# Attention sums moved by DMA into a transposed tile and divided there; norms that add the negated mean

## The chip, the core and the metric

The kernel runs on one core of a Trainium2 chip. The metric is the device time of one execution in microseconds, as the median over runs. TensorE is called PE in the profile, VectorE DVE, ScalarE ACT, GpSimd POOL; SP is the queue of SyncE, which issues every DMA of this kernel.

## The reference

Eight batches of 512 tokens with 256 channels pass through two attention layers and, after each, a tree-shaped feed-forward layer, all in float32. Each of the four parts starts with a layer norm and is added to the stream. The second attention is causal and rotates its queries and keys.

```python
def _layernorm(x, axis=-1, eps=1e-05):
    m = jnp.mean(x, axis=axis, keepdims=True)
    v = jnp.var(x, axis=axis, keepdims=True)
    return (x - m) / jnp.sqrt(v + eps)

# attention a (b: no biases, rotated q and k, causal mask), 16 heads of 16 channels
qkv = (jnp.einsum('bne,fe->bnf', x, qkv_w) + qkv_b).reshape(b, n, 3, HEADS, HEAD_DIM)
q, k, v = (qkv[:, :, 0], qkv[:, :, 1], qkv[:, :, 2])
scores = jnp.einsum('bnhd,bmhd->bhnm', q, k) / jnp.sqrt(jnp.float32(HEAD_DIM))
attn = jax.nn.softmax(scores, axis=-1)
out = jnp.einsum('bhnm,bmhd->bnhd', attn, v).reshape(b, n, EMBED)
return jnp.einsum('bne,fe->bnf', out, out_w) + out_b

# feed-forward: 255 gates, 256 leaf probabilities as products along the paths of a tree
gate = jax.nn.sigmoid(q_flat @ routers.T)
leaf_prob = _leaf_probs(gate)
ret = (leaf_prob @ leaf_values).reshape(Bv, Tv, d)
return jnp.einsum('btd,ed->bte', ret, Wout_w) + Wout_b

x = x + attention_a(_layernorm(x))
x = x + ffn(_layernorm(x))
x = x + attention_b(_layernorm(x))
x = x + ffn(_layernorm(x))
```

## The kernel before

The whole stream lies in SBUF, one tile per batch. There are 16 sequences of work, numbered n: 0 to 7 are the first attention of batches 0 to 7, 8 to 15 the causal one. The 16 heads of a sequence are handled in four groups g of four heads j; a group's four heads use four strips of 32 rows of the array.

The main loop counts half-steps: 32 per sequence, for each group four key tiles kt (or query tiles) in two pairs of heads. In a half-step the program emits `scores` for two heads (st, line 371), the row `maxima` of a later group for two heads (mx, line 334, twelve half-steps ahead), the `exponentials` (pt, line 381, ACT), and in every other half-step `weigh` (av, line 390), which multiplies the weights by v, a key tile behind. In the causal half an `affine_select` on POOL (line 523) cuts the diagonal block of pt before `weigh` may read it. v carries ones in 16 of its 32 columns, so av holds, per head, 16 rows of sums and 16 rows of the softmax's denominator.

`maxima` reduces each mx on DVE into a tile called less. When a group's less is complete, `put` transposes it (lessT, line 355), negates it on ACT (rows) and sends it by four small DMAs (q<-rows, line 360) into row 16 of each strip of q; the scores of that group then subtract the maximum by themselves, and must wait for these DMAs.

At a group's last key tile `weigh` copies av to SBUF (o, line 396), and a unit `divide` follows: four transposes on TensorE bring it to tokens by channels (oT, line 407), DVE takes the reciprocal of the denominators (inv, line 411) and multiplies (out, line 413). After the fourth group `post` transposes the whole of out back (outTp, line 245, 2 x 4 transposes with a copy on ACT to outT), multiplies it by the output weights (y, line 254) and adds it to x on DVE (line 423). Then `tree` runs the feed-forward layer: a norm, transposes (txt), gates (z), the products lp on DVE, transposes (lt), the leaves (ty), and an add to x.

`layer_norm` takes statistics on DVE (lines 224 and 225) and finishes on POOL: eps is added (line 229), the power taken (line 230), and four instructions form xn (line 233) as (x - mean) * rstd. `pre` is the front of the next sequence: norm, transposes (xt), q and k (line 282), rotation on POOL in the causal half (lines 302 to 306), DMAs that spread q and k over the strips (lines 294 and 310), and v.

Units are generators: each yields the kind of slot that it wants next ("pe" or "v") and a delay in half-steps. One unit of each kind is pulled per half-step, urgent ones first. On top of that a scheduler fixes each engine's final order when the program is built, so that an engine's order can differ from the program's. Each engine, SP's queue among them, takes its instructions in this order, and one that waits holds all behind it. SP's DMAs use eight semaphores in turn, and each waits for the eighth before it. PSUM has seven banks in rotation and one for av.

Of the kernel before, what the change touches and what calls it, by code (L numbers as in the profile page):

```python
# [31 lines left out]
F32 = mybir.dt.float32  # L35
AF = mybir.ActivationFunctionType
ALU = mybir.AluOpType
# [3 lines left out]
P = 128  # L41
B, S, D = 8, 512, 256
H, HD = 16, 16
NG, NJ = 4, 4
NT = S // P
NC = D // P
# [55 lines left out]
def hybrid_kernel(ctx, tc, x, a_qk, a_v, a_o, a_qk_b, a_v_b, a_o_b, b_q, b_k, b_v, b_o,  # L102
                  f_q, f_routers, f_values, f_out, f_out_b, cos, sin, leaf_scale, out):
    nc = tc.nc
# [27 lines left out]
    ident = const.tile([P, P], F32, tag="ident", name="ident")  # L132
# [19 lines left out]
    pool1 = ctx.enter_context(tc.tile_pool(name="w1", bufs=1))  # L152
    pool2 = ctx.enter_context(tc.tile_pool(name="w2", bufs=2))
# [5 lines left out]
                          (f_values, "f_values", "lp"), (f_out, "f_out", "lpT"))  # L159
    ]  # L160
    banks = ctx.enter_context(tc.tile_pool(name="banks", bufs=7, space=PSUM))
    ps_av = ctx.enter_context(tc.tile_pool(name="ps_av", bufs=1, space=PSUM))

    def bank(shape, name):
        return banks.tile(shape, F32, tag="ps", name=name)
# [11 lines left out]
    ks, vs, qs, outs, avs, lesses = [], [], {}, {}, {}, {}  # L177
    for i in range(2):
        k = pool1.tile([P, NG, S], F32, tag=f"k{i}", name=f"k{i}")
        v = pool1.tile([P, NT, H, 2 * HD], F32, tag=f"v{i}", name=f"v{i}")  # L180
# [5 lines left out]
    units = Units()  # L186
# [31 lines left out]
    def layer_norm(b, name, got):  # L218

        x = xs[b]  # L220
        stats = pool2.tile([P, NT, 6], F32, tag="ln_stats", name=f"ln_stats{name}")
        mv = pool2.tile([P, NT, 2], F32, tag="ln_mv", name=f"ln_mv{name}")
        for t in range(NT):
            nc.vector.bn_stats(stats[:, t, :], x[:, t, :])
            nc.vector.bn_aggr(mv[:, t, :], stats[:, t, :])  # L225
            if t % 2:
                yield "v", 0
        rstd = pool2.tile([P, NT], F32, tag="ln_rstd", name=f"ln_rstd{name}")
        nc.gpsimd.tensor_scalar(rstd, mv[:, :, 1], EPS, None, ALU.add)  # L229
        nc.gpsimd.tensor_tensor(rstd, rstd, neg_half, ALU.pow)  # L230
        xn = pool2.tile([P, NT, D], F32, tag="xn", name=f"xn{name}")
        for t in range(NT):
            nc.gpsimd.tensor_scalar(  # L233
                xn[:, t, :], x[:, t, :], mv[:, t, 0:1], rstd[:, t : t + 1], ALU.subtract, ALU.mult
            )
        got.append(xn)

# [3 lines left out]
    def transposed(dst, src, c, name):  # L241

        ps = bank([P, NT, P], name)
        for t in range(NT):
            nc.tensor.transpose(ps[:, t, :], src[:, t, c * P : (c + 1) * P], ident)  # L245
        nc.scalar.copy(dst[:, c, :], ps.rearrange("p t q -> p (t q)"))  # L246

    def by_tokens(srcT, w, n, tt, name):

        ps = bank([P, 2, D], name)  # L250
        for i in range(2):
            t = 2 * tt + i
            for c in range(NC):
                nc.tensor.matmul(  # L254
                    ps[:, i, :n], lhsT=srcT[:, c, t * P : (t + 1) * P], rhs=w[:, c, :],
                    start=c == 0, stop=c == NC - 1,
                )
        return ps

    def pre(n):  # L260

        causal, b = divmod(n, B)
        w = wb if causal else wa
        got = []
        yield from layer_norm(b, f"n{n}", got)
        xn = got[0]
        xnT = pool2.tile([P, NC, S], F32, tag="xnT", name=f"xnT{n}")
# [115 lines left out]
    def weigh(n, g, kt, pt):  # L383

        if kt == 0:
            avs[n, g] = ps_av.tile([P, S], F32, tag="av", name=f"av{n}_{g}")
        av = avs[n, g]
        first = kt * P if n >= B else 0
        for j in range(NJ):
            nc.tensor.matmul(  # L390
                av[32 * j : 32 * j + 32, first:], lhsT=vs[n % 2][:, kt, g * NJ + j, :],
                rhs=pt[:, j, : S - first], start=kt == 0, stop=kt == NT - 1,
            )
        if kt == NT - 1:
            o4 = pool2.tile([P, S], F32, tag="o4", name=f"o4{n}_{g}")
            nc.scalar.copy(o4, avs.pop((n, g)))
            units.add(divide(n, g, o4), "pe", 1, urgent=True)

    trees = {}

    def divide(n, g, o4):

        if g == 0:
            outs[n] = pool1.tile([P, NT, D], F32, tag="out", name=f"out{n}")
        ps = bank([P, NT, NJ, 2 * HD], f"oT{n}_{g}")
        for t in range(NT):
            nc.tensor.transpose(  # L407
                ps[:, t, :, :].rearrange("p j d -> p (j d)"), o4[:, t * P : (t + 1) * P], ident
            )
        inv = pool2.tile([P, NT, NJ, 1], F32, tag="inv", name=f"inv{n}_{g}")  # L410
        nc.vector.reciprocal(inv, ps[:, :, :, HD : HD + 1])
        to = outs[n].rearrange("p t (g j d) -> p t g j d", g=NG, j=NJ)
        nc.vector.tensor_tensor(
            to[:, :, g, :, :], ps[:, :, :, 0:HD], inv.to_broadcast([P, NT, NJ, HD]), ALU.mult
        )
        if g == NG - 1:
            trees[n] = units.add(post(n), "pe", 1)
        return
        yield

    def add_to_x(b, ps, tt):
        part = xs[b][:, 2 * tt : 2 * tt + 2, :]
        nc.vector.tensor_tensor(part, ps, part, ALU.add)  # L423

    def post(n):

        causal, b = divmod(n, B)
        outT = pool1.tile([P, NC, S], F32, tag="outT", name=f"outT{n}")
        out = outs.pop(n)
        for c in range(NC):  # L430
            transposed(outT, out, c, f"outTp{n}_{c}")
            yield "pe", 0
        for tt in range(NT // 2):
            add_to_x(b, by_tokens(outT, (wb if causal else wa).o, D, tt, f"y{n}_{tt}"), tt)
            yield ("v", 1) if tt else ("pe", 0)
        yield from tree(n, b)

    def tree(n, b):

        got = []
        yield from layer_norm(b, f"t{n}", got)
        xn = got[0]
        xnT = pool2.tile([P, NC, S], F32, tag="xnT", name=f"txnT{n}")
# [40 lines left out]
    def place(i, swapped):  # L486
        n, i = divmod(i, STEPS)
        g, i = divmod(i, 2 * NT)
        u, pair = divmod(i, 2)
        return n, g, u, pair ^ swapped  # L490
# [8 lines left out]
    for i in range(-LEAD, total + 2):  # L499
        ahead = i + LEAD  # L500
        if ahead < total:
            n, g, u, pair = place(ahead, 1)
# [15 lines left out]
        if got is not None:  # L518
            exponentials(sn, kt, got, pt)
            if sp == 1:  # L520
                if sn >= B:

                    nc.gpsimd.affine_select(  # L523
                        out=pt[:, :, :P], in_=pt[:, :, :P], pattern=[[0, NJ], [1, P]],
# [3 lines left out]
        if i % 2 and (len(waiting) > 1 or (i >= total and waiting)):  # L528
            weigh(*waiting.popleft())
# [64 lines left out]
```

## Time and profile before

| | |
|---|---|
| time, median of 3 runs | 1599.61 us (1596.56 to 1602.42) |
| the profiled execution | 1595.46 us |
| its span, first to last instruction | 1593.7 us |
| mean granted clock of TensorE | 0.862 of full speed |
| PE busy | 1481.2 us (93%) |
| DVE, ACT, POOL busy | 757.5, 665.9, 453.8 us |
| DMA traffic of the queue q1 | 24736 packets, 29.64 MB |

The page gives for each engine the time in which it had an instruction at work, and a picture of the span in 40 slices, each digit a share in tenths. PEclk is the clock that TensorE was granted. A row of a group of instructions ends with the mean ns of one, the idle time just before them and what ended it. A row of waits reads: who waited, at which line, for whom; total us, times, longest. A row of the timeline reads: start, length, engine, line, operation, output and inputs, how many in a row, and in brackets the idle time before it with its releaser. A window row gives its length, the busy us and count of PE, PEld, DVE, ACT and POOL, then the granted clock, the DMA share and GB/s.

### The profile page before, as it was taken

To read this page: it belongs to the slowest core of one execution; us is meant where nothing else is said; L and a number is where in the kernel's file an instruction comes from. 1 tells how busy PE (TensorE), PEld (TensorE's weight loads), DVE (VectorE), ACT (ScalarE), POOL (GpSimd) and SP (SyncE) were. 2 spreads that over 40 slices of the span, in tenths; PEclk is the share of its full clock that TensorE was granted. 3 is DMA by queue.
4 is the path that set the end of the run, shared out by engine and by line. 5 is a ranking of instruction groups with operands and counts; after the bars stand their busy time and mean duration, and the time that the engine had idled before them with its cause. 6 is when DMAs were issued, how large, how long until landed. Compare 5 with 4: busy or idle time off the path is not lost.

```text
span 1593.7 us, 22833 instructions
## 1 busy us (share of the span) xinstructions
PE 1481.2 (93%) x8276; PEld 668.1 (42%) x8276; DVE 757.5 (48%) x2247; ACT 665.9 (42%) x1443; POOL 453.8 (28%) x452
## 2 busy tenths in 40 slices
PE   4999999999999999999998898989889798989895
PEld 2333444334344434433444444445445343445444
DVE  2355655546546555455544343544444344544422
ACT  1155545445445444545454342534334343433331
POOL 7000300402104040032416245451624445251312
PEclk9599999889799988979999596977979787986767
DMA  7001001000010100100101000000101001010000
GB/s 230 17 11 18 11 1 27 2 17 12 2 27 1 28 1 1 28 1 8 22 1 28 1 14 15 23 19 14 28 1 32 10 23 19 15 28 2 14 14 13
DMA packets 24847, 31.09 MB, mean 20 GB/s; under 512 B 4000, under 2 KB 16032, under 8 KB 24736
## 3 DMA queue, kind: packets, MB, share of 16 engines
q1 hardware_dynamic: 24736, 29.64, 7.9%
q8 instruction: 66, 1.08, 0.3%
q14 instruction: 45, 0.37, 0.1%
HBM read 8.13 MB, written 4.19 MB: 8 GB/s over the span
## 4 chain that ended last, share of the span: by engine, by line
PE 84%; POOL 7%; DVE 6%; issue 1%; ACT 1%; DMA 1%; SPq 0%; POOLq 0%; DVEq 0%; ACTq 0%
PE st L371 26%; PE av L390 15%; PE mx L334 10%; PE qk L282 8%; PE z L254 5%; PE ty L254 4%; PE v L254 4%; PE y L254 4%; DVE lp L471 3%; POOL xnt L233 2%; POOL xnn L233 2%; PE oT L407 2%; PE txt L245 2%; PE lt L245 2%; PE outTp L245 1%
## 5 line engine op out<-in xcount | busy, mean ns | idle before, releaser
L381 ACT ACTIVATE pt<-st 128x512 f32<-128x512 f32 (+3 forms) x1024 | 473.7, 517 | 488.1 <-PE mx L334 413.8
L334 PE MATMUL mx<-k,q 16*128 16x512 f32 (+3 forms) x2048 | 623.5, 631 | 6.1 <-issue 6.1
L371 PE MATMUL st<-q,k 17*128 17x512 f32 (+3 forms) x2048 | 565.2, 619 | 33.4 <-DMA q<-rows 29.6
L348 DVE TENSOR_REDUCE less<-mx 128x1 f32<-128x512 f32 x512 | 328.5, 684 | 301.0 <-PE mx L334 300.3
L343 DVE CUSTOM_DVE_ANT_0 seen<-mx,mask 128x512 f32<-128x512 f32 (+3 forms) x512 | 230.7, 487 | 340.5 <-PE mx L334 331.2
L390 PE MATMUL av<-pt,v 128*32 128x512 f32 (+3 forms) x2048 | 272.3, 608 | 27.9 <-POOL pt L523 27.8
L371 PEld LDWEIGHTS st<-q,k 17*128 17x128 f32 x2048 | 183.6, 208 | 232.9 <-issue 152.2
L334 PEld LDWEIGHTS mx<-k,q 16*128 16x128 f32 x2048 | 219.5, 209 | 58.5 <-ACT pt L381 28.5
L523 POOL TENSOR_SCALAR_AFFINE_SELECT pt<-pt 128x512 f32<-128x512 f32 x128 | 81.6, 640 | 431.8 <-ACT pt L381 431.1
L229 POOL TENSOR_SCALAR ln_rstdt<-ln_mvt 128x4 f32<-128x4 f32 x16 | 3.7, 232 | 592.9 <-DVE ln_mvt L225 592.9
L390 PEld LDWEIGHTS av<-pt,v 128*32 128x32 f32 x2048 | 43.0, 115 | 199.8 <-issue 139.5
L254 PE MATMUL z<-wg,txnT 128*128 128x255 f32 x256 | 79.7, 466 | 0.5 <-ACT txnT L246 0.5
L233 POOL TENSOR_SCALAR xnt<-x,ln_mvt,ln_rstdt 128x256 f32<-128x256 f32 x64 | 77.4, 1221 | 0.3
L233 POOL TENSOR_SCALAR xnn<-x,ln_mvn,ln_rstdn 128x256 f32<-128x256 f32 x64 | 77.4, 1220 | 0.1
L254 PE MATMUL ty<-wl,lpT 128*128 128x256 f32 x256 | 73.1, 436 | 0.0
L254 PEld LDWEIGHTS z<-wg,txnT 128*128 128x128 f32 x256 | 57.2, 235 | 35.6 <-issue 10.9
L282 PE MATMUL qk<-xnT,a_qk 128*128 128x512 f32 x128 | 68.0, 661 | 0.0
L254 PEld LDWEIGHTS ty<-wl,lpT 128*128 128x128 f32 x256 | 52.5, 216 | 32.0 <-DVE x L423 8.3
L471 DVE SCALAR_TENSOR_TENSOR lp<-th,lp 128x8 f32<-128x8 f32 (+6 forms) x224 | 64.0, 322 | 3.3
L302 POOL TENSOR_TENSOR by_cos<-eo,cos 128x512 f32<-128x512 f32 x32 | 40.7, 1270 | 80.4 <-ACT eo L287 80.4
L407 PE MATMUL oT<-ident,o 128*128 128x128 f32 x256 | 47.2, 313 | 10.6 <-DVE less L343 7.8
L407 PEld LDWEIGHTS oT<-ident,o 128*128 128x128 f32 x256 | 30.4, 155 | 58.6 <-ACT pt L381 20.9
(74 smaller groups left out, 1143.8 us busy)
## 6 DMA issues: line engine op xcount, KB each, us to landing
x<-x SPq DMA_DIRECT2D x8, 512.0 KB
q<-r SPq DMA_DIRECT2D x32, 128.0 KB
k<-r SPq DMA_DIRECT2D x32, 128.0 KB
q<-rows SPq DMA_DIRECT2D x256, 2.0 KB
q<-rot SPq DMA_DIRECT2D x64, 64.0 KB
k<-rot SPq DMA_DIRECT2D x64, 64.0 KB
out<-x SPq DMA_DIRECT2D x8, 512.0 KB
a_qk<-a_qk SPq DMA_DIRECT2D x1, 512.0 KB
```

What stands on the lines that cost most here:

```text
L233: nc.gpsimd.tensor_scalar(xn[:, t, :], x[:, t, :], mv[:, t, 0:1], rstd[:, t : t + 1], ALU.subtract, ALU.mult)
L254: nc.tensor.matmul(ps[:, i, :n], lhsT=srcT[:, c, t * P : (t + 1) * P], rhs=w[:, c, :], start=c == 0, stop=c == NC - 1,)
L282: nc.tensor.matmul(ps, lhsT=wt[:, k, c * P : (c + 1) * P], rhs=xnT[:, k, :], start=k == 0, stop=k == NC - 1,)
L334: nc.tensor.matmul(ps[:, :width], lhsT=qs[n][rows, g, qt * P : (qt + 1) * P], rhs=ks[n % 2][rows, g, :width], start=True, stop=True,)
L343: nc.vector.tensor_tensor_reduce(out=seen[:, :width], in0=ps[:, :width], in1=mask[:, S - width :], scale=1.0, scalar=LOWEST, op0=ALU.add, ...
L348: nc.vector.tensor_reduce(at, ps, AX.X, ALU.max)
L371: nc.tensor.matmul(ps[:, : S - first], lhsT=ks[n % 2][rows, g, kt * P : (kt + 1) * P], rhs=qs[n][rows, g, first:], start=True, stop=True,)
L381: nc.scalar.activation(pt[:, j, :width], ps[:, :width], AF.Exp, scale=SCALE)
L390: nc.tensor.matmul(av[32 * j : 32 * j + 32, first:], lhsT=vs[n % 2][:, kt, g * NJ + j, :], rhs=pt[:, j, : S - first], start=kt == 0, stop= ...
L407: nc.tensor.transpose(ps[:, t, :, :].rearrange("p j d -> p (j d)"), o4[:, t * P : (t + 1) * P], ident)
L471: nc.vector.scalar_tensor_tensor(pairs[:, :, :, side], of_level, one, lp, ALU.add, ALU.mult)
L523: nc.gpsimd.affine_select(out=pt[:, :, :P], in_=pt[:, :, :P], pattern=[[0, NJ], [1, P]], compare_op=ALU.is_ge, fill=0.0, base=0, channel_m ...
```

## The change

`weigh` no longer hands o to a unit on TensorE. It allocates three tiles per sequence, outT (channels by tokens, two halves c), den of the same shape, and few, and issues eight DMAs per group: for each head, one that folds the 512 denominators of one row into 16 partitions of 32 (few), and one that copies the 16 rows of sums to their place in outT. After the second and the fourth group a unit `divide` takes the reciprocal of few on DVE, writes it to a DRAM tile by one DMA (apart), and reads it back by eight DMAs, each of which spreads one head's 512 reciprocals over 16 partitions (den). One slot later POOL multiplies outT by den in place. `post` then starts with the output product. The transposes oT and outTp, the copies to outT and the products on DVE are gone.

In `layer_norm` a new POOL instruction forms the negated mean, and xn is computed as (x + negated mean) * rstd.

The lines of the file after move down by two to six.

```diff
+    dram = ctx.enter_context(tc.tile_pool(name="apart", bufs=2, space=bass.MemoryType.DRAM))
...
+        less_mean = pool2.tile([P, NT], F32, tag="ln_less", name=f"ln_less{name}")
+        nc.gpsimd.tensor_scalar(less_mean, mv[:, :, 0], -1.0, None, ALU.mult)
         rstd = pool2.tile([P, NT], F32, tag="ln_rstd", name=f"ln_rstd{name}")
...
             nc.gpsimd.tensor_scalar(
-                xn[:, t, :], x[:, t, :], mv[:, t, 0:1], rstd[:, t : t + 1], ALU.subtract, ALU.mult
+                xn[:, t, :], x[:, t, :], less_mean[:, t : t + 1], rstd[:, t : t + 1], ALU.add, ALU.mult
             )
...
             nc.scalar.copy(o4, avs.pop((n, g)))
-            units.add(divide(n, g, o4), "pe", 1, urgent=True)
+            if g == 0:
+                outs[n] = [pool1.tile([P, NC, S], F32, tag=t, name=f"{t}{n}") for t in ("outT", "den")]
+                outs[n].append(pool2.tile([P, NC, S // HD], F32, tag="few", name=f"few{n}"))
+            outT, den, few = outs[n]
+            c = g // 2
+            for j in range(NJ):
+                to = slice((g % 2) * 64 + HD * j, (g % 2) * 64 + HD * (j + 1))
+                nc.sync.dma_start(few[to, c, :], o4[32 * j + HD : 32 * j + HD + 1, :])
+                nc.sync.dma_start(outT[to, c, :], o4[32 * j : 32 * j + HD, :])
+            if g % 2:
+                units.add(divide(n, c), "v", 2, urgent=True)
...
-    def divide(n, g, o4):
-
-        if g == 0:
-            outs[n] = pool1.tile([P, NT, D], F32, tag="out", name=f"out{n}")
-        ps = bank([P, NT, NJ, 2 * HD], f"oT{n}_{g}")
-        for t in range(NT):
-            nc.tensor.transpose(
-                ps[:, t, :, :].rearrange("p j d -> p (j d)"), o4[:, t * P : (t + 1) * P], ident
-            )
-        inv = pool2.tile([P, NT, NJ, 1], F32, tag="inv", name=f"inv{n}_{g}")
-        nc.vector.reciprocal(inv, ps[:, :, :, HD : HD + 1])
-        to = outs[n].rearrange("p t (g j d) -> p t g j d", g=NG, j=NJ)
-        nc.vector.tensor_tensor(
-            to[:, :, g, :, :], ps[:, :, :, 0:HD], inv.to_broadcast([P, NT, NJ, HD]), ALU.mult
-        )
-        if g == NG - 1:
+    def divide(n, c):
+        outT, den, few = outs[n]
+        inv = pool2.tile([P, S // HD], F32, tag="inv", name=f"inv{n}_{c}")
+        nc.vector.reciprocal(inv, few[:, c, :])
+        apart = dram.tile([H // NC, S], F32, tag="apart", name=f"apart{n}_{c}")
+        nc.sync.dma_start(apart.rearrange("h (a r) -> (h a) r", a=HD), inv)
+        for h in range(H // NC):
+            nc.sync.dma_start(den[HD * h : HD * (h + 1), c, :], apart[h : h + 1, :].to_broadcast([HD, S]))
+        yield "v", 2
+        nc.gpsimd.tensor_tensor(outT[:, c, :], outT[:, c, :], den[:, c, :], ALU.mult)
+        if c == NC - 1:
             trees[n] = units.add(post(n), "pe", 1)
...
-        outT = pool1.tile([P, NC, S], F32, tag="outT", name=f"outT{n}")
-        out = outs.pop(n)
-        for c in range(NC):
-            transposed(outT, out, c, f"outTp{n}_{c}")
-            yield "pe", 0
+        outT = outs.pop(n)[0]
```

More of the change, by code (lines that the diff above doesn't have):

```diff
@@ L396, in weigh @@
             nc.scalar.copy(o4, avs.pop((n, g)))
-            units.add(divide(n, g, o4), "pe", 1, urgent=True)
-    trees = {}
-    def divide(n, g, o4):
-        if g == 0:
-            outs[n] = pool1.tile([P, NT, D], F32, tag="out", name=f"out{n}")
-        ps = bank([P, NT, NJ, 2 * HD], f"oT{n}_{g}")
-        for t in range(NT):
-            nc.tensor.transpose(
-                ps[:, t, :, :].rearrange("p j d -> p (j d)"), o4[:, t * P : (t + 1) * P], ident
-            )
-        inv = pool2.tile([P, NT, NJ, 1], F32, tag="inv", name=f"inv{n}_{g}")
-        nc.vector.reciprocal(inv, ps[:, :, :, HD : HD + 1])
-        to = outs[n].rearrange("p t (g j d) -> p t g j d", g=NG, j=NJ)
-        nc.vector.tensor_tensor(
-            to[:, :, g, :, :], ps[:, :, :, 0:HD], inv.to_broadcast([P, NT, NJ, HD]), ALU.mult
-        )
-        if g == NG - 1:
+            if g == 0:
[9 more added lines that the diff above has]
+                units.add(divide(n, c), "v", 2, urgent=True)
+    trees = {}
+    def divide(n, c):
[9 more added lines that the diff above has]
+        if c == NC - 1:
             trees[n] = units.add(post(n), "pe", 1)
-        return
-        yield
     def add_to_x(b, ps, tt):
```

## The prediction

> **What bounds the kernel now.** I read the page's busy rows first, then TensorE's own waits, then the stretches where it waits. PE is TensorE, PEld its weight loads, DVE VectorE, ACT ScalarE, POOL GpSimd, SP the queue that issues every DMA.
>
> ```profile
> PE 1481.2 (93%) x8276; PEld 668.1 (42%) x8276; DVE 757.5 (48%) x2247; ACT 665.9 (42%) x1443; POOL 453.8 (28%) x452
> PE   4999999999999999999998898989889798989895
> PEclk9599999889799988979999596977979787986767
> ...
> PE st L371 <- DMA q<-rows: 29.6, 7, 4.4
> PE av L390 <- POOL pt L523: 27.8, 8, 5.2
> ```
>
> TensorE is the bound: full through the first, non-causal half, full but for some 10% in the causal half. What it waits for there is named in the two rows (total us, times, longest): a row of negated maxima that comes by DMA, and pt behind POOL. The window table gives 702.66 us busy of 770 from 750 to 1520. One causal sequence shows both waits:
>
> ```profile
> 861.15 6.10 SPq L310 DMA_DIRECT2D k<-rot  x8
> 867.29 20.45 SPq L360 DMA_DIRECT2D q<-rows  x5
> 868.70 4.84 POOL L233 TENSOR_SCALAR xnt<-x,ln_mvt,ln_rstdt 128x256 f32<-128x256 f32 x4
> 871.64 1.19 PE L371 MATMUL st<-q,k 17*128 17x512 f32 x1 [4.21 <-DMA q<-rows]
> 881.31 1.93 PE L390 MATMUL av<-pt,v 128*32 128x512 f32 x8 [3.65 <-POOL pt L523]
> ```
>
> The fourth q<-rows DMA stood in SP's queue behind eight k<-rot DMAs, and TensorE stood 4.21 us. Then pt's affine_select stood on POOL behind 15 us of norms, and TensorE stood 3.65 us. So two in-order queues, SP and POOL, set the stalls, and the change puts work into both.
>
> A gap costs more than its length:
>
> ```profile
> 410.00:415.00 5.00, 5.00 (x32) 2.40 (x30) 2.60 (x15) 2.66 (x5) 0.00 (x0) 1.00 0.00 2
> 415.00:420.00 5.00, 4.24 (x32) 1.75 (x24) 5.00 (x10) 2.23 (x4) 0.00 (x0) 0.93 0.00 0
> 420.00:425.00 5.00, 5.00 (x24) 1.43 (x20) 1.79 (x4) 1.67 (x3) 0.00 (x0) 0.50 0.00 0
> 435.00:440.00 5.00, 5.00 (x20) 1.63 (x18) 1.36 (x3) 1.44 (x3) 0.00 (x0) 0.52 0.01 3
> 440.00:445.00 5.00, 5.00 (x30) 2.78 (x28) 2.67 (x4) 1.08 (x2) 0.00 (x0) 1.00 0.00 0
> ```
>
> The column after POOL's is the granted clock. After 0.76 us of idle it is 0.50 for some 20 us. In windows of 2 us nearly every stretch with 1.2 us or more of idle in the causal half is followed by 14 to 30 us at 0.5; some such stretches also begin with no gap.
>
> **The change, part by part.** The sum is made against the profiled execution, 1595.46 us (span 1593.7, 1.8 around it); the median of the runs is 4.1 us above it.
>
> *Removed.* 256 oT and 128 outTp transposes:
>
> ```profile
> L407 PE MATMUL oT<-ident,o 128*128 128x128 f32 x256 | 47.2, 313 | 10.6 <-DVE less L343 7.8 <-DVE less L348 1.4 <-ACT o L396 1.2
> L245 PE MATMUL outTp<-ident,out 128*128 128x128 f32 x128 | 21.8, 296 | 0.0
> L360 SPq DMA_DIRECT2D q<-rows x256: 572/573/968, 68.2 to 1530.4; - x128
> ```
>
> 47.2 + 21.8 = 69.0 us of TensorE, 4.3 us per sequence (16 of them), all on the path in the first half. The ACT copies to outT (18.8 us) and the DVE products (27.2 us) go too, but those engines are half idle, so they count nothing. In the last sequence the cover of TensorE is gone, and there the old route was short: o copied at 1554.5, y begun at 1557.4.
>
> *Added on SP.* Eight DMAs per (n, g), nine per (n, c): 512 + 288 = 800, beside 448 of its kind now (256 rows, 64 r, 128 rot). At the row's 573 ns (600 on average in a run of four) that is 460 us of issuing, in bursts of 4.8 us and 5 us, each ahead of some q<-rows. From issue to landing no row gives a plain number. Bounds: four rows issued from 402.01 move their bytes from 403 to 406, so about 2 us; the one behind k<-rot took 4.3; the final 512 KB store issued at 1589.96 was awaited 2.3 us. I take 2.
>
> *c = 0, first half.* In DVE's order the reciprocal stands before the last reduction of less_3, so lessT_3 on TensorE waits for it, and it for the four few DMAs. Let o be copied at T. SP issues few and outT in turn; the last few starts at T+3.7 and lands at T+5.7; reciprocal 0.25, reduction 0.68: lessT_3 at T+6.8. TensorE, with the transposes gone and xt moved elsewhere, has two half-steps of st and mx (1.0 each), one av (1.06) and half of another, and DVE its lp work: about T+4.4. Stall 2.4. Behind it SP: apart T+6 to 6.6, landed at 8.6; eight dens to 13.4; four rows, the first landed at T+15.5. st_3_0 is reached near T+14: 1.5 more.
>
> *c = 1, first half.* k<-r and three of four rows go before the dens; the last den lands near T+17, POOL's product (1.27, by the row by_cos, 128x512) ends at T+18.5, and y is reached between T+16 and T+18. I take 1 us, bounds 0 and 2.7. The norm after it starts later: 0.5.
>
> *Causal.* c = 0: the reciprocal holds the same reductions, and POOL's product stands before the affine_select of pt_2_2, waiting for the dens: 3.5 us. c = 1: SP's order is one q<-rot (waits for POOL's rot, T+3), eight few and outT (to T+8), seven q<-rot (to T+13), apart, three rows, eight dens (T+16 to T+20.6), the fourth row. The product ends at T+23; TensorE is at y near T+14: 9 us, where now there are 4.2. Then POOL has y's norm, the bias and the next norm ahead of pt_1_1: 2.2 + 15.7 us (0.5 of it the two new less_mean instructions at 0.23) against 10.5 us of TensorE work at about 0.9 clock: 6.4, where now there are 3.6. So +5 and +2.8.
>
> *The negated mean.* xn takes 1221 ns for 256 columns. The nearest rows say that the kind of operation does not matter: rot by subtract 1266, by add 1267. I take no change. [...] If add leaves the slow route, an estimate at the affine_select's 640 ns is 0.58 x 4 = 2.3 us per norm, two norms per causal sequence: up to -35.
>
> *Clock.* [...] The trace decides: gaps from 1 us on, 20 us at half, so 10 us of full-speed work where TensorE is the bound. In the first half the c = 0 stall is such a gap in each sequence and the c = 1 stall in about half; the present slow stretches (106 us from 150 to 750, 8 us lost per sequence) are partly replaced: +6. In the causal half already 39 of 93 us are slow: +3.
>
> Sum: first half 8 x (-4.3 + 3.9 + 1.5 + 6) = +57. Causal 7.5 x (-4.3 + 3.5 + 5 + 2.8 + 3) = +75. End: o to y by the new route is 4.8 + 2 + 0.3 + 2.6 + 4.8 + 2 + 1.3 - overlaps of 1.7 = 16 us against 3, the clock aside: +12 net of the transposes. +144: 1739; with the 4.1 us to the median 1743, said as 1740.
>
> **The rivals.** *Faster: the chains hide.* The c = 0 wait decides from the point where TensorE takes longer than 6.8 us from o to lessT_3. At half clock it takes 8.8, st_3_0 moves back too, and the removed transposes count. If slow stretches or later DVE work cover these places, what is left is -69 + 12: 1543. For it: DVE had been busy without a break around such a place (513.6 to 523.1). Against: the granted clock is 0.92 from 150 to 750, and the causal waits are there already. Chance 0.09.
>
> *No clock price.* The stalls come, but the stretches at half clock only move: 8 x 1.1 + 7.5 x 7 + 12 = +73: 1673. For it: slow stretches begin at 234 and 310 without a gap. Chance 0.22.
>
> *The negated mean pays.* All as forecast and -35: about 1705; with no clock price 1638. [...] against it rot. Chance 0.2.
>
> *About the same.* Hidden chains in the first half and longer stalls in the causal half cancel: 0.03. The forecast itself: 0.46.
>
> **How the numbers follow.** 1740 is the likeliest case. The low end takes in no clock price with the negated mean; the high end has two slow stretches per first-half sequence (+8 each) and 5 more in the causal ones: 1840. Range 1625 to 1840; the faster case lies outside. What a measurement of this kernel can tell from no change is about 0.3%, 5 us. Slower 0.88, same 0.03, faster 0.09.
>
> **What would show it.** In the profile after: oT and outTp gone; 800 more SP issues; TensorE waiting for lessT_3 behind DVE's inv, for st_3_0 behind rows, for y behind POOL's product; a lower PEclk in the first half; xn still at 1.22 us. Wrong would be: few landing within 3 us of o's copy, den within 12, no y waits over 2 us in causal sequences, or a clock of 0.92 or more in the first half.

## The result, and the profile after

The changed kernel takes 1755.82 us (median of 4 runs, 1738.66 to 1766.08), beside 1601.01 us (1596.56 to 1624.03) for the kernel before on the same chip. The ratio is 1.094, 95% interval 1.084 to 1.105. The profiled execution is the longest of the four, 1766.08 us (span 1764.4); its granted clock is 0.765, where the others have 0.77 to 0.78. Some executions of a kernel run over 1.5% longer at a lower granted clock (of 15 of the kernel before, the longest 1624.44 us at 0.841, the shortest 1580.69 at 0.872); medians here are over all executions and ratios over the others alone, so that a ratio is not the quotient of two medians.

From the page, TensorE's busy row and two rows of the 40 slices:

```profile
PE 1606.3 (91%) x7892; PEld 679.2 (38%) x7892; DVE 736.6 (42%) x2151; ACT 650.4 (37%) x1411; POOL 419.4 (24%) x516
...
PE   5999999999999999999998888989888897989984
...
PEclk8555969769797886888968686676878777787576
```

TensorE has 384 instructions fewer and is busy 125 us longer. In the first half it is as full as it was, in digits all 9, but PEclk now falls in the middle of the nines. That is the reading to learn: a busy row says that there was an instruction, not how fast it ran.

TensorE's waits (total us, times, longest), and those of the reciprocal:

```profile
PE av L395 <- POOL pt L529: 49.0, 22, 4.0
PE y L259 <- POOL outT L427: 41.7, 9, 14.0
...
PE lessT L360 <- DVE less L348: 16.5, 7, 3.1
...
PE lessT L360 <- DVE less L353: 7.1, 5, 2.9
...
PE st L376 <- DMA q<-rows: 0.5, 2, 0.4
```

```profile
DVE inv L421 <- DMA few<-o: 92.7, 24, 11.9
```

The waits that the prediction named are there, lessT behind DVE and y behind POOL's product; the one for q<-rows has gone (29.6 us before). But windows of 2 us show that between 150 and 750 us TensorE is idle for 6.1 us only (2.8 before), while the clock there is 0.803 (0.920 before): 118 us of full-speed work are lost to it, where 48 were.

Where that happens is seen by listing TensorE's instructions other than st, mx and av. First the kernel before, a timeline and windows of 5 us (the columns as above, the clock third from the end):

```profile
485.75 2.00 PE L254 MATMUL y<-a_o,outT 128*128 128x256 f32 x8
...
495.11 0.66 PE L407 MATMUL oT<-ident,o 128*128 128x128 f32 x4
...
502.78 0.66 PE L245 MATMUL txt<-ident,xnt 128*128 128x128 f32 x4
```

```profile
490.00:495.00 5.00, 5.00 (x32) 1.53 (x28) 4.41 (x10) 2.76 (x5) 4.16 (x6) 1.00 0.00 0
495.00:500.00 5.00, 5.00 (x35) 2.01 (x33) 3.46 (x7) 2.58 (x5) 5.00 (x5) 1.00 0.00 0
500.00:505.00 5.00, 5.00 (x32) 1.90 (x28) 2.59 (x5) 2.96 (x7) 5.00 (x4) 1.00 0.02 5
```

Then the kernel after, the same place of a sequence:

```profile
532.19 2.86 PE L259 MATMUL y<-a_o,outT 128*128 128x256 f32 x12
...
540.30 1.12 PE L376 MATMUL st<-q,k 17*128 17x512 f32 x2 [0.41 <-DVE less L353]
...
550.14 1.12 PE L250 MATMUL txt<-ident,xnt 128*128 128x128 f32 x4
...
558.30 2.92 PE L259 MATMUL z<-wg,txnT 128*128 128x255 f32 x8
```

```profile
534.00:539.00 5.00, 5.00 (x34) 2.07 (x33) 4.84 (x16) 1.62 (x3) 0.28 (x2) 1.00 0.00 0
539.00:544.00 5.00, 4.59 (x24) 1.30 (x23) 4.46 (x11) 2.17 (x4) 4.72 (x7) 0.92 0.10 21
544.00:549.00 5.00, 5.00 (x21) 1.68 (x17) 2.39 (x4) 2.31 (x5) 4.65 (x8) 0.50 0.05 11
549.00:554.00 5.00, 5.00 (x24) 1.95 (x16) 0.80 (x3) 1.29 (x3) 2.40 (x2) 0.50 0.00 1
554.00:559.00 5.00, 5.00 (x20) 1.49 (x19) 1.96 (x4) 2.03 (x4) 0.00 (x0) 0.50 0.00 0
559.00:564.00 5.00, 5.00 (x24) 3.25 (x22) 1.29 (x2) 1.68 (x3) 0.00 (x0) 0.88 0.00 0
```

From the end of y (535) to the first txt (550) TensorE executes st, mx and av alone (and one lessT, a narrow one): products that the trace shows as `17*128` (st), `16*128` (mx) and `128*32` (av), where y and txt are `128*128`. Eight microseconds into this stretch the clock halves, 3 us after one idle of 0.41 us, and it is full again only in z, 17 us later, though TensorE is busy for 5.00 of 5 us. In the kernel before, oT stands in the middle of the same stretch. Call the instructions of `128*128` (y, z, ty, qk, v and the 128 x 128 transposes) whole-array work. From 170 to 760 us of the changed kernel's trace eleven stretches between whole-array work are 13 us or longer, and the clock falls in all eleven.

The other unexpected line is in the norms (the kernel before had 77.4 us and 1221 ns in each such row):

```profile
L238 POOL TENSOR_SCALAR xnt<-x,ln_lesst,ln_rstdt 128x256 f32<-128x256 f32 x64 | 34.9, 558 | 1.8
```

### The profile page after: what moved, and what is told of

The parts are those of the page before. It is cut to its first block, busy times and chain, and to the rows that moved or that the text cites. A ratio compares the mean times of both kernels' runs of the same rounds, so it can differ in the third digit from the quotient of the medians.

```text
span 1764.4 us, 23322 instructions
## 1 busy us (share of the span) xinstructions
PE 1606.3 (91%) x7892; PEld 679.2 (38%) x7892; DVE 736.6 (42%) x2151; ACT 650.4 (37%) x1411; POOL 419.4 (24%) x516
## 4 chain that ended last, share of the span: by engine, by line
PE 74%; SPq 8%; DMA 5%; DVE 5%; POOL 5%; issue 2%; ACT 1%; ACTq 0%; DVEq 0%; POOLq 0%
PE st L376 24%; PE av L395 13%; PE mx L339 9%; PE qk L287 5%; PE ty L259 5%; PE y L259 4%; PE z L259 4%; PE v L259 3%; SPq L315 2%; DVE lp L477 2%; SPq L410 2%; PE lt L250 2%; DMA apart<-inv 2%; SPq L425 2%; PE txt L250 2%
## 5 line engine op out<-in xcount | busy, mean ns | idle before, releaser
L339 PE MATMUL mx<-k,q 16*128 16x512 f32 (+3 forms) x2048 | 683.9, 700 | 8.9 <-DMA k<-r 8.4
L376 PE MATMUL st<-q,k 17*128 17x512 f32 (+3 forms) x2048 | 637.0, 689 | 6.9 <-DVE less L348 3.8
L395 PE MATMUL av<-pt,v 128*32 128x512 f32 (+3 forms) x2048 | 311.6, 686 | 49.1 <-POOL pt L529 49.0
L376 PEld LDWEIGHTS st<-q,k 17*128 17x128 f32 x2048 | 202.6, 226 | 280.0 <-issue 158.7
L339 PEld LDWEIGHTS mx<-k,q 16*128 16x128 f32 x2048 | 234.9, 227 | 73.9 <-issue 31.6
L427 POOL TENSOR_TENSOR outT<-outT,den 128x512 f32<-128x512 f32 x32 | 41.0, 1282 | 696.6 <-DMA q<-rows 315.3
L259 PE MATMUL y<-b_o,outT 128*128 128x256 f32 x128 | 53.1, 575 | 37.8 <-POOL outT L427 37.8
L259 PEld LDWEIGHTS ty<-wl,lpT 128*128 128x128 f32 x256 | 60.6, 249 | 44.0 <-issue 11.3
L433 DVE TENSOR_TENSOR x<-y,x 128x512 f32<-128x512 f32 x32 | 22.0, 688 | 89.9 <-PE y L259 89.8
L433 DVE TENSOR_TENSOR x<-ty,x 128x512 f32<-128x512 f32 x32 | 22.1, 692 | 88.3 <-PE ty L259 88.3
L259 PEld LDWEIGHTS y<-b_o,outT 128*128 128x128 f32 x128 | 34.8, 290 | 57.2 <-POOL outT L427 45.3
```

Of the source, the lines that this page charges most:

```text
L259: nc.tensor.matmul(ps[:, i, :n], lhsT=srcT[:, c, t * P : (t + 1) * P], rhs=w[:, c, :], start=c == 0, stop=c == NC - 1,)
L339: nc.tensor.matmul(ps[:, :width], lhsT=qs[n][rows, g, qt * P : (qt + 1) * P], rhs=ks[n % 2][rows, g, :width], start=True, stop=True,)
L376: nc.tensor.matmul(ps[:, : S - first], lhsT=ks[n % 2][rows, g, kt * P : (kt + 1) * P], rhs=qs[n][rows, g, first:], start=True, stop=True,)
L395: nc.tensor.matmul(av[32 * j : 32 * j + 32, first:], lhsT=vs[n % 2][:, kt, g * NJ + j, :], rhs=pt[:, j, : S - first], start=kt == 0, stop= ...
```

## Experiments

All ratios are to the kernel before, run beside each kernel on the same chip. The two halves are read from the first and last y of each profiled execution: the first half from the first y of sequence 0 to the last start of y in sequence 7, the causal half from there to the last start of y. The halves, the clocks and the waits come from one profiled execution of each kernel, which can lie up to 24 us from the kernel's median (the negated mean alone: 1554.13 us), so a few us between two halves say nothing by themselves.

| kernel | median us | ratio, 95% interval | clock 150 to 750 us | first half us | causal half us |
|---|---|---|---|---|---|
| before | 1601 | 1 | 0.920 | 686.9 | 697.8 |
| after | 1755.82 | 1.094 (1.084 to 1.105) | 0.803 | 753.5 | 774.8 |
| negated mean alone | 1578.06 | 0.984 (0.969 to 1.000) | 0.932 | 679.1 | 671.1 |
| route alone | 1769.66 | 1.115 (1.106 to 1.124) | 0.801 | 757.8 | 786.9 |
| no route | 1614.33 | 1.016 (1.008 to 1.024) | 0.896 | 675.1 | 721.7 |
| idle DMAs | 1613.51 | 1.008 (1.003 to 1.013) | 0.936 | 678.7 | 704.0 |
| transposes put back | 1705.03 | 1.067 (1.053 to 1.081) | 0.888 | 708.5 | 765.6 |
| after, filled | 1694.89 | 1.059 (1.048 to 1.071) | 0.871 | 717.4 | 767.2 |
| later divide | 1714.54 | 1.074 (1.060 to 1.089) | 0.887 | 706.7 | 757.5 |
| fixed den | 1639.14 | 1.033 (1.026 to 1.040) | 0.890 | 676.7 | 734.1 |
| no route, filled | 1595.06 | 1.000 (0.996 to 1.005) | 0.942 | 650.0 | 731.4 |
| before, filled | 1549.44 | 0.978 (0.970 to 0.986) | 0.952 | 671.9 | 674.9 |
| the same, rows by ScalarE | 1577.87 | 0.990 (0.986 to 0.994) | 0.949 | 680.5 | 691.2 |
| before, filled more | 1542.54 | 0.968 (0.959 to 0.978) | 0.972 | 671.5 | 656.3 |

### The negated mean alone, and the route alone

```diff
 # in the kernel before
+        less_mean = pool2.tile([P, NT], F32, tag="ln_less", name=f"ln_less{name}")
+        nc.gpsimd.tensor_scalar(less_mean, mv[:, :, 0], -1.0, None, ALU.mult)
...
-                xn[:, t, :], x[:, t, :], mv[:, t, 0:1], rstd[:, t : t + 1], ALU.subtract, ALU.mult
+                xn[:, t, :], x[:, t, :], less_mean[:, t : t + 1], rstd[:, t : t + 1], ALU.add, ALU.mult
```

> The kernel before, with the negated mean alone. After's profile has xn at 558 ns by add, where subtract took 1221, so each norm's xn group is 2.65 us shorter on GpSimd, less 0.24 for the new instruction. If GpSimd's norms ahead of pt's affine_select set the causal half's waits (27.8 us of av behind pt, and y's chain), about 4.8 us of the queue go in each causal sequence and some 2 to 4 us of that reach the end: 1565 to 1585 us. Rival: q<-rot and k<-rot in SP's queue set the causal half anyway, and av's wait is only moved: 1595 to 1602.

The second kernel is the changed one with these lines the other way round.

> The changed kernel with xn by subtract again and no negated mean: the new route of the attention's sums alone. If the negated mean was worth in the changed kernel what the queue of GpSimd says (4.8 us per causal sequence, all of it behind y, since POOL's product, y's norm and the next norm follow each other there), this is 30 to 40 us above the changed kernel: 1785 to 1795 us. If the clock is what costs and not GpSimd's queue, it is within 10 us of it: 1755 to 1765.

Alone the negated mean gives 0.984, with an interval that just touches 1; from the route alone to the change the ratio falls from 1.115 to 1.094, about 33 us. Two comparisons on different work point to a gain, of about 25 and 33 us, each known to some 25 us. By the ratio the route alone meets its expectation of 30 to 40 us above the change; by its median, 1769.66 us, it lies only 14 us above it, between the two expectations. Most of the gain lies in the causal half of the profiled executions (697.8 to 671.1 us, and 786.9 to 774.8), where the norms stand ahead of pt's affine_select. TensorE's waits with the negated mean alone:

```profile
PE st L373 <- DMA q<-rows: 29.8, 7, 4.4
...
PE av L392 <- POOL pt L525: 3.5, 2, 2.8
```

av's wait for POOL has gone from 27.8 to 3.5 us, the one for q<-rows stayed.

### No route

```diff
-            for j in range(NJ):
...
-                nc.sync.dma_start(few[to, c, :], o4[32 * j + HD : 32 * j + HD + 1, :])
-                nc.sync.dma_start(outT[to, c, :], o4[32 * j : 32 * j + HD, :])
...
-        nc.vector.reciprocal(inv, few[:, c, :])
...
-        nc.gpsimd.tensor_tensor(outT[:, c, :], outT[:, c, :], den[:, c, :], ALU.mult)
+    fixed = pool1.tile([P, NC, S], F32, tag="outT", name="fixed")     # y reads this
```

> The changed kernel without the route: the eight DMAs of each group, the reciprocal, its write and its spreading, and POOL's product are left out; the output product reads a tile that was filled once with a part of x, so the attention's sums do not reach the output. TensorE's work is that of the changed kernel. Theory A (waits behind the new chain start the slow stretches of the clock): the 69 us of transposes are really saved, the clock from 150 to 750 us is back at 0.90 to 0.93, and with the shorter norms the time is 1490 to 1520 us. Theory B (without the transposes TensorE's own work is granted less clock): the slow stretches stay with no wait ahead of them, clock 0.80 to 0.83 from 150 to 750 us, and the time is 1580 to 1640 us.

This run decides most. With no DMAs of the route, no reciprocal, no product and 69 us less on TensorE, the kernel is slower than before, 1.016, and by 0.031, some 50 us, slower than the kernel with the negated mean alone, which does all that work. In the first half, where y waits for nothing, the saving is 4 us (679.1 to 675.1) instead of 34: the clock is 0.896 instead of 0.932 with TensorE idle for 0.3 us in 600. All six stretches of 15 us and more without whole-array work there (z to lt) lose the clock, two of them only in their last 2 us; the six of 12.0 us (y to txt), without a gap in them, keep it. So theory B holds for the first half: the time lies in its range, though the clock, 0.896, is nearer to A's 0.90 than to B's 0.80 to 0.83; six stretches lose it here, eleven in the changed kernel. In the causal half something else adds to it:

```profile
PE av L398 <- POOL pt L518: 56.7, 16, 6.1
PE lessT L363 <- DVE less L351: 14.0, 7, 2.0
```

y comes earlier relative to the other work, the fixed orders put both norms (and the rotation) on POOL ahead of the affine_select of pt_1_0 instead of pt_2_0, and TensorE waits for it up to 6.1 us in each sequence.

### Idle DMAs

```diff
 # the kernel before, old route kept
+                nc.sync.dma_start(few[to, c, :], o4[32 * j + HD : 32 * j + HD + 1, :])
+                nc.sync.dma_start(idleT[to, :], o4[32 * j : 32 * j + HD, :])
...
+        nc.sync.dma_start(apart.rearrange("h (a r) -> (h a) r", a=HD), few[:, c, :])
+        for h in range(H // NC):
+            nc.sync.dma_start(den[HD * h : HD * (h + 1), :], apart[h : h + 1, :].to_broadcast([HD, S]))
```

> The kernel before, with the changed kernel's 800 DMAs added at the same places of SP's queue, into tiles that nothing but these DMAs reads (the spread values are undivided sums of weights; den and outT hold one half at a time). Transposes and the old route stay; no engine waits for the new DMAs except SP, and q<-rows, q<-rot and k<-rot stand behind them. Theory A (DVE's, SP's and GpSimd's waits on the chain are the cost): only the part through SP remains, the rows behind the dens, about 1.5 us per half of a sequence and the clock after it: 1615 to 1650 us. Theory C (the traffic itself, 800 issues and 29000 packets, is the cost): a rise like the changed kernel's own without its saving, 1750 to 1830 us. If both are off the path: 1600 us.

800 DMAs and 29000 packets cost 1.008, some 13 us: theory C falls. The waits for q<-rows rise from 29.6 to 39.2 us, the only clear trace of the crowding of SP's queue in TensorE's waits.

### The transposes put back, and filling

```diff
 # in the changed kernel
+            units.add(turn(n, g, o4), "pe", 1, urgent=True)     # four transposes of o4, unused
...
+            for t in range(NT):                                # in post, ahead of y
+                nc.tensor.transpose(ps[:, t, :], xs[b][:, t, c * P : (c + 1) * P], ident)
```

> The changed kernel, with as many transposes as the old route had put back on TensorE at the old places (four of o per group, eight before y, of a part of x), their results unused. In the first half of the changed kernel's trace the granted clock halves 6 to 9 us after the last instruction that is not st, mx, av or lessT, and such stretches last 16 to 21 us; in the kernel before, oT cuts them to 7 to 13 us. Theory B (the stretches without whole-array work are what halves the clock; oT had broken them): clock from 150 to 750 us up from 0.80 to 0.88 or more, and although TensorE has 69 us of instructions more at full clock, the time does not rise: 1700 to 1755 us. Theory A (the waits behind the new chain start the slow stretches): clock unchanged, the transposes come on top: 1805 to 1825 us.

```diff
 # in scores
+            if j == 2 * pair and lean[0] >= 2:      # half-steps since the last unit of TensorE
+                for t in range(4):
+                    nc.tensor.transpose(ps[:, t * P : (t + 1) * P], ident, ident)
+                lean[0] = 0
```

> The changed kernel, with four transposes of the identity ahead of an st wherever two half-steps have passed without a unit of TensorE: 65 groups, some 0.6 us each, 39 us in all, written where the st then overwrites them; no buffer, wait or DMA is added. Theory B: the clock from 150 to 750 us goes from 0.80 to 0.88 or more, of the 118 us lost there half comes back, and the time is 1680 to 1730 us. Theory A: clock unchanged, 1780 to 1800 us.

> The kernel without the route (1614 us; its sums do not reach the output), with four transposes of the identity ahead of an st wherever two half-steps have passed without a unit of TensorE: 65 groups, 39 us at full clock; the order of all else stays. Removing the old transposes was worth nothing there although 69 us of TensorE's work went. Theory B (their place was taken by half-clock stretches): clock from 150 to 750 us up from 0.896 to 0.94 or more, and the 39 us come for nothing or better: 1580 to 1615 us, the saving of the removal still not reached. If the loss is only that y and its norm now stand earlier in GpSimd's order (av behind pt 56.7 us in the causal half): the groups come on top, 1640 to 1655 us.

Three times work was added that nobody uses, and three times the kernel got faster. With 384 more transposes the ratio falls from 1.094 to 1.067; with 65 groups of the identity from 1.094 to 1.059; the kernel without the route goes from 1.016 to 1.000. PEclk of the kernel with the transposes put back, beside the row of after above:

```profile
PEclk9776979798998898979987876967769587787776
```

The second pair adds no buffer and no wait, and the transposes are overwritten where they stand, so what changes is TensorE's own activity. In all three pairs the clock from 150 to 750 us rose with the whole-array work added: from 0.803 to 0.888 and to 0.871, and from 0.896 to 0.942. (The profiled executions of the two filled kernels took about 20 us more than their medians, so that their clocks are, if anything, read too low.) The kernel without the route tells what the removal is worth once the clock is higher (0.942): its first half is 650.0 us, 29 below the negated mean alone and 22 below the kernel before when that is filled too (671.9, below), where the transposes take 34. The causal half, 731.4, keeps av's waits behind POOL (46.8 us).

### Fixed den

```diff
-        nc.vector.reciprocal(inv, few[:, c, :])
+        nc.vector.reciprocal(inv, ones[:, : S // HD])
...
-        nc.gpsimd.tensor_tensor(outT[:, c, :], outT[:, c, :], den[:, c, :], ALU.mult)
+        nc.gpsimd.tensor_tensor(outT[:, c, :], outT[:, c, :], ones, ALU.mult)
```

> The changed kernel with all its DMAs, but the reciprocal and POOL's product read a tile of ones, so that neither waits for few or den (the sums stay undivided); the order of instructions stays. What is tried is the price of these two waits with what they start. If the route's cost over the kernel without it (1.094 against 1.016 of the kernel before) lies in the waits: lessT's and y's waits go below 10 us and the time falls to 1620 to 1650 us. If it lies in the traffic, SP's order and the places of the instructions: 1720 to 1760 us. By theory B alone the first half stays near a clock of 0.80 to 0.85, since the stretches without whole-array work stay as long, but each begins without a wait.

1.033 instead of 1.094: the two dependences are worth 0.061, some 98 us. With the waits gone the fixed orders shift a little too (y runs as two whole groups of eight; in the changed kernel its twelve last instructions wait together), so this is the price of the dependences with what the order makes of them. TensorE's waits:

```profile
PE av L395 <- POOL pt L531: 56.2, 17, 6.1
...
PE lessT L360 <- DVE less L348: 14.0, 7, 2.0
PE y L259 <- POOL outT L429: 7.8, 1, 7.8
```

Idle of TensorE from 150 to 750 us is 6.2 us, as in the changed kernel (6.1), and yet the first half is 77 us shorter. What the dependences cost there is the clock (0.890 here, 0.803 in the changed kernel): y to txt now takes 12.0 us with no gap in three of the first five sequences, and keeps it; in the changed kernel a gap of 0.41 us stands some 5 us into it, the clock falls 1 to 3 us later, and at half speed the stretch grows to some 16. lessT's 14.0 us are not the route's: the kernel without it has the same row.

The first sequence, ahead of the first y and so outside the 77 us, is another matter. The changed kernel has no whole-array work from 90.7 to 167.5 us, and the clock is at half for all but 5 us of it, though TensorE waits for nothing there. With fixed den it is at half just as long, 78.5 us in each kernel, so this loss is not the dependences'. One window of each, the changed kernel first:

```profile
120.00:121.00 1.00, 1.00 (x8) 0.73 (x7) 0.78 (x2) 0.87 (x2) 0.00 (x0) 0.50 0.00 0
...
120.00:121.00 1.00, 1.00 (x5) 0.20 (x8) 0.69 (x1) 0.25 (x1) 0.00 (x0) 0.50 0.24 39
```

So theory A is right that the waits carry most of the route's price, and theory B, whose own forecast of 0.80 to 0.85 for the clock missed here (0.890), names the way in which a short wait comes to cost so much.

### Later divide

```diff
-                units.add(divide(n, c), "v", 2, urgent=True)
+                units.add(divide(n, c), "v", 5, urgent=True)
...
-        yield "v", 2
+        yield "v", 4
```

> The changed kernel with the delays of divide raised from 2 and 2 half-steps to 5 and 4: the reciprocal is placed later in DVE's order, and POOL's product and y later still, so that the few and den DMAs have landed when their readers are reached. Theory A (waits on the chain and the slow stretches that they start): lessT and y no longer wait, the time falls towards that of the kernel without the route, 1620 to 1670 us. Theory B (whole-array work is missing between y and the gates): the first half keeps its clock of 0.80 and its 104 us per sequence, only the causal waits of y (41.7 us) and of av behind pt (49 us) shrink: 1700 to 1745 us.

1.074, where theory A expected 1620 to 1670 us. y waits 19.3 us instead of 41.7 and av behind pt 11.5 instead of 49.0, but lessT still waits (11.5 and 8.3), and the row on top is a new one:

```profile
PE st L376 <- DMA q<-rows: 86.2, 8, 12.1
```

A wait went from POOL to SP, whose queue now has the dens and the rotated q and k ahead of rows. In the first half the clock rises to 0.887, where theory B expected 0.80, but y's instructions now stand apart and cut the stretches, so this run doesn't separate the theories there.

### A version that beats both

```diff
 # the kernel before, with the negated mean and, in scores:
+            if j == 2 * pair and lean[0] >= 2:      # >= 1 in the second kernel
+                for t in range(4):
+                    nc.tensor.transpose(ps[:, t * P : (t + 1) * P], ident, ident)
```

> The kernel before with the negated mean, and four transposes of the identity ahead of an st wherever two half-steps have passed without a unit of TensorE: 24 groups, 14 us of TensorE's time. Theory B: the stretches of 8 to 13 us around oT that still halve the clock are cut, 41 us lost from 150 to 750 us go to 25 or less and some of the causal half's go too: 1550 to 1570 us, a little under the negated mean alone (1578). Theory A: the clock does not care, 1585 to 1595 us.

> The kernel before with the negated mean and four transposes of the identity ahead of an st in every second half-step without a unit of TensorE: 89 groups instead of 24, 53 us of TensorE's time at full clock. Theory B: more of the 29 us lost from 150 to 750 us and of the 104 us from 750 to 1450 us comes back, but the groups cost about as much: 1530 to 1570 us. If the clock's loss in the causal half is from its gaps and not from these stretches: 1580 to 1600 us.

0.978 with 24 groups and 0.968 (0.959 to 0.978) with 89: 1542.54 us, 45 us below the kernel before in its rounds. PEclk with 89 groups, whose 53 us of extra work (the figure expected) go with a clock from 150 to 750 us of 0.972 instead of the 0.932 of the negated mean alone:

```profile
PEclk9699999999999999999999698896989798996987
```

The remaining wait for q<-rows was attacked too, with `nc.scalar.dma_start` in `put` of the kernel with 24 groups:

> The kernel before with the negated mean and the 24 groups of transposes (1549 us), with the q<-rows DMAs issued by ScalarE, right behind the instruction that makes rows, instead of SP, where eight k<-rot stand ahead of the fourth: st's waits for rows (24.5 us, once per causal sequence, each at the start of a slow stretch of some 25 us) should go. If these gaps start the slow stretches: 1480 to 1520 us. If ScalarE's issuing [...] delays pt, or the stretches without whole-array work keep the clock low anyway: 1530 to 1570 us.

It went the wrong way, 0.990 instead of 0.978, and 1577.87 us lies outside both expectations. The wait for rows is gone, and av waits for POOL instead:

```profile
PE av L396 <- POOL pt L530: 37.2, 9, 5.4
```

## Why the prediction was right in its total, and where its steps failed

Along four kernels the change is a sum: negated mean -25 us (0.984), transposes removed +50 (to 1.016), DMAs and product without their dependences +28 (to 1.033), the dependences with what follows +98 (to 1.094). That is +151; the medians differ by 155. Each term has an uncertainty of some 15 to 25 us.

*Removed, -69 us: the step that failed most.* It took TensorE's seconds as saved because TensorE is the bound. TensorE had 69 us less to do, but in the first half 4 us of 34 came, and in the causal half time was lost. The instructions were whole-array work in the middle of stretches of narrow products. With the clock raised by filling (0.942), 22 to 29 of the 34 do come.

*Negated mean, "no change": wrong.* The step went by rot, where add and subtract take the same 1.27 us; but rot is another kind of instruction. xn fell to 558 ns, below the affine_select's 640 that the prediction's rival used, and that rival's 35 us are near what was measured (about 25 and 33).

*The waits: right in place, too large.* The route was costed at +213 (the sum of 144 and the 69 removed); from the kernel without it to the changed one it is 125. Without the clock the waits and the end make about 140 of the 213 (8 x 5.4, 7.5 x 11.3 and 12), but TensorE's idle time rose by 46 us only (112.5 to 158.1, each the span less the busy time). The queues behaved as read: few and outT take 0.59 us each and come in bursts of 5 us, in the first half the last few is mostly issued 3.8 us after o's copy (forecast 3.7), lessT_3 comes 6.5 to 8.7 us after it in the first half (forecast 6.8), and y's last wait, the tail, is 14.0 us against 16. What was wrong is how early TensorE arrives. The wait for rows behind the dens (1.5 us per sequence) is 0.5 us in all. lessT_3 of the first half waits 1.2 us at most, not 2.4, and in three of the eight sequences not at all; the clock there is at half in part, the point that the rival that the chains hide named. And y in the causal half waits 3.4 us per sequence, not 9 (41.7 less 14.0 at the end and 4.0 in the first half, over 7). Here both places on the time line were right; the step took y as one piece. In the sequence whose o is copied at 1137.8:

```profile
1152.36 0.70 PE L259 MATMUL y<-b_o,outT 128*128 128x256 f32 x2
...
1160.28 1.26 POOL L427 TENSOR_TENSOR outT<-outT,den 128x512 f32<-128x512 f32 x1 [2.03 <-DMA q<-rows]
...
1161.60 5.49 PE L259 MATMUL y<-b_o,outT 128*128 128x256 f32 x12 [2.91 <-POOL outT L427]
```

TensorE is at y 14.5 us after the copy (forecast 14) and the product ends at 23.7 (forecast 23), but the first four instructions (this pair, and one more at 1154.0) read the half that is ready, and st, mx and av fill most of the time until the other twelve.

*Clock: right in sign, too small, and put down to gaps alone.* The step had +6 us per sequence in the first half and +3 in the causal one, some 70 in all, started by gaps of 1 us. Measured: 118 against 48 us lost in the 600 us from 150 to 750, 12 per sequence of about 100 us; and 212 against 130 in the causal stretches (850 to 1700, and 750 to 1520 before), 10 per sequence. Over the two spans some 195 us more are lost (0.138 of 1593.7, 0.235 of 1764.4). The step's 106 slow us of the kernel before count every window of 2 us that is not wholly at full clock; at half are 96. Idle time does not account for it: in the changed kernel the clock was 0.50 with 5.00 of 5 us busy (three windows, 544 to 559), and without the route it was 0.896 from 150 to 750 us with 0.3 us of idle in all. The start, before 150 us, was not costed at all: the first y comes 29.6 us later (206.5, not 176.9).

So the total came out near by luck. By the runs, an imagined saving of 69 us, really a loss of 50, stood against a route counted 88 us too high and a gain of 25 to 33 us left out. By the trace, waits and end were put 94 us too high and the clock's price some 125 us too low. The case "no clock price", 1673, is excluded by the runs: filling alone gives back 0.035 with every wait in place.

No run varied the share of the array in use by itself, so that the clock follows this share was not shown; that it rose when whole-array work was added was, three times (0.803 to 0.888 and 0.871, 0.896 to 0.942). The +28 of DMAs and product were not taken apart; in the profiled executions 22 us of the difference lie ahead of the first y (177.8 and 199.7), and why is open.

## What to carry to other kernels

Before removing work from a TensorE that is always busy, look at the granted clock around it and at what is left between the remaining wide instructions: here a stretch of narrow products ran at half clock though its busy row was full (0.50 with 5.00 of 5 us busy), and a few transposes there were worth more than they took (65 groups, 39 us by the estimate on record, brought the ratio from 1.094 to 1.059). The busy row alone does not tell: the changed kernel has 5.00 of 5 us busy at 1.00 (534 to 539) and at 0.50 (544 to 549). The chain of small DMAs cost little by its traffic (1.008 with 800 that nobody waits for), and much by the in-order engines that stand and wait for its end (1.094, against 1.033 without the two dependences). When one wait is lifted by moving a DMA or a unit, look for the next queue that it lands in: the later divide took 22.4 us from y's wait, and st waited 86.2 us for q<-rows.

## What the runs showed of the hardware

- TensorE's clock fell to 0.50 with next to no idleness: without the route it was 0.896 from 150 to 750 us, with 0.3 us of idle. Over the first halves (170 to 760 us) of six traces (before, after, each part alone, no route, idle DMAs), of the stretches between whole-array work that began at full clock, all 29 of 13 us or longer lost it, of 128 shorter ones (3 to 13 us) 28 did, most of them 5 to 8 us after the last whole-array instruction. Length alone does not tell: near the start, from 88 to 135 us, the kernel before has three such stretches of 14.8 to 15.9 us at 1.00.
- In the changed kernel the clock, once at 0.50 (from 543.2 us), stayed there for 17 us with TensorE busy throughout, two groups of txt at 550.1 and 553.2 among its work, and was at 1.00 again within z (559 to 564: 0.88). What the clock goes by was not shown.
- With 24 groups of four 128 x 128 transposes added to the kernel with the negated mean alone, the clock from 150 to 750 us was 0.952, with 89 groups 0.972, where it was 0.932 without them. Such a group took 0.66 us at full clock (oT at 495.11).
- GpSimd's tensor_scalar on 128 x 256 takes 1221 ns as subtract and multiply with the mean read from a strided tile, and 553 to 558 ns as add and multiply with the negated mean from a dense one; the two differences were not tried apart. Its tensor_tensor on 128x512 takes 1.27 us as add and as subtract.
